# Tiles of x for layer 1 kept beside the projection's tiles and asked for earlier

## The chip, the cores and the metric

The kernel runs on one core of a Trainium2 chip. The metric is the time of one execution on the device in microseconds; the median of five executions is given, and one more was profiled. The core has five engines with queues of their own: PE (TensorE, matmuls, with PEld for its weight loads), DVE (VectorE), ACT (ScalarE), POOL (GpSimd) and SP (SyncE, here only a queue from which transfers are issued). Transfers are also issued from ACT and POOL; all of them share 16 DMA engines.

## The reference

The input x is one image of 48 channels by 256 x 256. Two layers, each adding to x what it computes from a group-normalised x (`_gn`: 16 groups of 3 channels, mean and variance over the whole image).

```
# layer 0
qkv = dwconv3x3(einsum('bchw,oc->bohw', _gn(x), w_qkv))     # 144 channels
q, k, v = heads(split(qkv))        # 4x4 patches: 8 heads, 96 values per patch
attn = softmax(l2norm(q)^T l2norm(k) * temperature)         # 4356 x 4356 per head, padding's border included
x = x + einsum(fold(v attn^T), w_proj)                      # the projection
# layer 1
xb = _gn(x) cut into windows of 64 x 64
x = x + einsum('bcphqw,twW,thH,tcC->bCpHqW', xb, Ws, Hs, Cs)   # t = 0, 1, 2
```

## The kernel before

All data are float32. Layer 0 goes through statistics of x, the pointwise and depthwise convolutions and the attention of eight heads; that takes the first 3227 of 3705 us. Attention's matmuls lie in a hand-ordered loop. At its end the sums of the last head are transposed and stored to DRAM in the tensor `os_` (`store`, L609 to L619, from POOL), which has 16 parts; each covers 256 patches.

**The projection** (L726 to L762) goes over 8 tiles t. One tile takes 16 rows of the upper half of the image and 16 rows of the lower half, on 96 partitions. For each tile SP loads `pot` (`os_`, parts t and 8 + t, L740) and `pxt` (x itself, L741), two loads each, 768 KB apiece. PE multiplies `pot` with the projection weights (L746), DVE adds the result onto `pxt` (L753) and takes statistics of it (L757), and POOL stores the rows to `x1s` in DRAM (L762, two stores). `pot` and `pxt` have three buffers each, in the pool `pj`. Behind the loop come the group statistics for layer 1, then its channel weights `csn` scaled by them (L782) and a bias `cbias` (L788).

**Layer 1** goes over 8 units: a unit is one row of windows (64 image rows) by one half of the image's width (128 columns). For each unit `load_x` loads `lxq` (two loads of 768 KB from `x1s`, 32 rows each on 48 partitions, L815) and `load_rows` loads the same data once more in another layout for the residual (`lrt`, L824). `over_c` (L828) contracts the channels on PE (L841); DVE subtracts `cbias` and writes the tile `lzt` (L848). `over_w` contracts the width with `wsb` (L863), `over_h` the height with `hsb` (L880), `residual` adds (L892) and stores to the output (L895). The units are worked on in a hand-ordered block: `load_x` for units 0 and 1 and `over_c(0)` first, then each unit with `load_x` of the unit after next and `over_c` of the next one woven into it.

**Order.** Instructions outside the hand-ordered blocks are put into an order on each engine's queue by a planner: one that is ready goes, and among several ready ones the one written earlier. On its queue each instruction then waits for the semaphores that it needs.

**Places in SBUF.** Pools are stacked in the order in which they are opened; a pool that has been closed leaves its place to later ones, and a first tile there waits for those who used it. Per partition: attention had `cv` (52 KB), `ahead` with the key, query and value tiles (80 KB), then the pool of the `e` tiles (48 KB), then small ones. In their place the projection opens `l1c` (1 KB), `pj` (`pot` 48 KB, then `pxt` 48 KB) and `pjs` (3 KB). When these two are closed, layer 1 opens `lx` (48 KB, three `lxq`), `lz` (`wsb`, `hsb`, two `lzt`; 74 KB), `lr` (24 KB) and `ly` (24 KB) from the same address on as `pj`: `lxq` lies on `pot`, `wsb` and the first `lzt` on `pxt`.

Of the kernel before, what the change touches and what calls it, by code (L numbers as in the profile page):

```python
# [8 lines left out]
F32 = mybir.dt.float32  # L9
# [4 lines left out]
PSUM = bass.MemoryType.PSUM  # L14
DRAM = bass.MemoryType.DRAM

C = 48
H = W = 256
# [23 lines left out]
WS = 64  # L42
# [3 lines left out]
def conv_preact_kernel(  # L46
# [15 lines left out]
    nc = tc.nc  # L62
# [16 lines left out]
    x1s = dram.tile([C, H, W], F32, name="x1s")  # L79
# [18 lines left out]
    for s in range(2):  # L98
        r = slice(s * C, (s + 1) * C)
        for h in range(NH if s == 0 else H0):  # L100
            o = s * M0 + h * HC if h < H0 else (h - H0) * HC
            nc.gpsimd.dma_start(
                out=(wq[r] if h < H0 else wr[0:C])[:, o : o + HC].rearrange("c (z e) -> c z e", z=3),
                in_=w_qkvT.rearrange("c (z h e) -> h c z e", z=3, h=NH)[h],
# [22 lines left out]
    def group_stats(st, mean, rstd, pool, pspool):  # L127

        mv = pool.tile([P2, 2], F32, name="mv")
        nc.vector.bn_aggr(mv, st.rearrange("p n s -> p (n s)"))  # L130
        pm = pspool.tile([P2, 1], F32, name="pm", tag="pstat")
        nc.tensor.matmul(pm, lhsT=gm, rhs=mv[:, 0:1], start=True, stop=True)
        nc.vector.tensor_copy(mean, pm)
        d = pool.tile([P2, 1], F32, name="gsd")
        nc.vector.tensor_sub(d, mv[:, 0:1], mean)
        e = pool.tile([P2, 1], F32, name="gse")
        nc.vector.scalar_tensor_tensor(e, d, d, mv[:, 1:2], ALU.mult, ALU.add)
        pv = pspool.tile([P2, 1], F32, name="pv", tag="pstat")
        nc.tensor.matmul(pv, lhsT=gm, rhs=e, start=True, stop=True)
        f = pool.tile([P2, 1], F32, name="gsf")  # L140
        nc.vector.tensor_scalar_add(f, pv, EPS)
        g = pool.tile([P2, 1], F32, name="gsg")
        nc.scalar.activation(g, f, AF.Sqrt)
        nc.vector.reciprocal(rstd, g)
        return mv, e
# [257 lines left out]
    with tc.tile_pool(name="xn", bufs=1) as xnp, tc.tile_pool(name="cst", bufs=1) as cst, tc.tile_pool(  # L403
        name="nps", bufs=2, space=PSUM
# [7 lines left out]
        parts = [16] * 7 + [8, 4, 4]  # L412
        st0 = cst.tile([P2, HALF * W // 512, 6], F32, name="st0")
        for i, LR in enumerate(parts):
            j = sum(parts[:i])
            for s in range(2):
                eng = nc.sync if s == 0 else nc.scalar
                eng.dma_start(
                    out=xr[s * C : (s + 1) * C, j : j + LR, :], in_=xc[:, s * HALF + j : s * HALF + j + LR, :]
# [70 lines left out]
    with tc.If(nc.values_load(large) > 0):  # L490
# [8 lines left out]
        with tc.tile_pool(name="mk", bufs=NM) as mk, tc.tile_pool(name="mq", bufs=2) as mq, tc.tile_pool(  # L499
            name="mps", bufs=2, space=PSUM  # L500
# [23 lines left out]
    with tc.tile_pool(name="ahead", bufs=2) as ah, tc.tile_pool(name="ae", bufs=3) as ae, tc.tile_pool(  # L524
        name="asm", bufs=6
# [109 lines left out]
        with tc.manual_schedule():  # L635
            load_query(0, 1)
            block = scores(0, 0)
            for h in range(NH):
                more = h + 1 < NH
                rows = {r: Depthwise(h + 1, r) for r in range(CR + 1)} if more else {}  # L640
                for g in range(NG):
# [57 lines left out]
                    for k in range(NK):  # L699
                        s = (h * NG + g) * NK + k  # L700
# [25 lines left out]
    l1c = ctx.enter_context(tc.tile_pool(name="l1c", bufs=1))  # L726
    RP = TP // PX * KS
    NP = TP
    with tc.tile_pool(name="pj", bufs=3) as pj, tc.tile_pool(name="pjs", bufs=1) as pjs, tc.tile_pool(
        name="pps", bufs=3, space=PSUM  # L730
    ) as pps, tc.tile_pool(name="pp1", bufs=1, space=PSUM) as pp1:
        st1 = pjs.tile([P2, HALF * W // 512, 6], F32, name="st1")
        ov = os_.rearrange("t (c k) n -> t c k n", k=KK)
        for t in range(HALF // RP):
            ot = pj.tile([P2, KK, NP], F32, name="pot")
            xt = pj.tile([P2, RP, W], F32, name="pxt")
            for s in range(2):
                r = slice(s * C, (s + 1) * C)
                y0 = s * HALF + t * RP
                nc.sync.dma_start(out=ot[r], in_=ov[s * (NT // 2 // TP) + t])  # L740
                nc.sync.dma_start(out=xt[r], in_=xc[:, y0 : y0 + RP, :])  # L741
            xv = xt.rearrange("p (py ki) (px kj) -> p ki kj py px", ki=KS, kj=KS)
            for ki in range(KS):
                ps = pps.tile([P2, KS, NP], F32, name="pps")
                for i in range(0, KS, 2):
                    nc.tensor.matmul(  # L746
                        ps[:, i : i + 2, :],
                        lhsT=wp,
                        rhs=ot[:, ki * KS + i : ki * KS + i + 2, :],
                        start=True,  # L750
                        stop=True,
                    )
                nc.vector.tensor_add(  # L753
                    xv[:, ki], ps.rearrange("p k (py px) -> p k py px", py=RP // KS), xv[:, ki]
                )
            for i in range(0, RP, 2):
                nc.vector.bn_stats(  # L757
                    st1[:, (t * RP + i) // 2, :], xt[:, i : i + 2, :].rearrange("p a b -> p (a b)")
                )
            for s in range(2):  # L760
                y0 = s * HALF + t * RP
                nc.gpsimd.dma_start(out=x1s[:, y0 : y0 + RP, :], in_=xt[s * C : (s + 1) * C])  # L762

        gm2 = pjs.tile([P2, 64 + C], F32, name="gm2")
        nc.vector.memset(gm2, 0.0)
        for o in (0, 64):
            nc.vector.tensor_copy(gm2[:, o : o + C], gm[:, 0:C])
        mv1, e1 = group_stats(st1, mean1, rstd1, pjs, pp1)
        pc1 = pp1.tile([64 + C, 1], F32, name="pc1", tag="pstat")
        nc.tensor.matmul(pc1, lhsT=gm2, rhs=e1, start=True, stop=True)  # L770
        rstd2 = l1c.tile([64 + C, 1], F32, name="rstd2")
        nc.vector.tensor_scalar_add(rstd2, pc1, EPS)
        nc.scalar.activation(rstd2, rstd2, AF.Sqrt)
        nc.vector.reciprocal(rstd2, rstd2)

        csn = l1c.tile([64 + C, T3 * C], F32, name="csn")
        for s in range(2):
            nc.scalar.dma_start(
                out=csn[s * 64 : s * 64 + C].rearrange("c (t d) -> c t d", t=T3), in_=Cs.rearrange("t c d -> c t d")
            )  # L780
            r = slice(s * 64, s * 64 + C)
            nc.vector.tensor_scalar_mul(csn[r], csn[r], rstd2[r])  # L782
        mrow = pjs.tile([C, 128], F32, name="mrow")
        nc.vector.tensor_scalar_mul(mrow, ones, mean1[0:C])
        pb1 = pp1.tile([128, T3 * C], F32, name="pb1")
        nc.tensor.matmul(pb1, lhsT=mrow, rhs=csn[0:C], start=True, stop=True)
        cbias = l1c.tile([128, T3 * C], F32, name="cbias")
        nc.vector.tensor_copy(cbias, pb1)  # L788


    with tc.tile_pool(name="lx", bufs=3) as lx, tc.tile_pool(name="lz", bufs=2) as lz, tc.tile_pool(
        name="lr", bufs=2
    ) as lr, tc.tile_pool(name="ly", bufs=4) as ly, tc.tile_pool(name="ps1", bufs=2, space=PSUM) as ps1, tc.tile_pool(
        name="ps2", bufs=2, space=PSUM
    ) as ps2, tc.tile_pool(name="ps3", bufs=1, space=PSUM) as ps3:
        wsb = lz.tile([128, T3, 128], F32, name="wsb", bufs=1)
# [2 lines left out]
        for s in range(2):  # L799
            r = slice(s * WS, (s + 1) * WS)  # L800
            nc.scalar.dma_start(out=wsb[r, :, r], in_=Ws.rearrange("t w v -> w t v"))
            nc.scalar.dma_start(out=hsb[r], in_=Hs.rearrange("t h g -> h t g"))
        HW = WS // 2
        units = [(yw, xh) for yw in range(H // WS) for xh in range(2)]
        NQ = 3
        xqs, rts, zts, blks, parts = {}, {}, {}, {}, {}

        def load_x(u):

            yw, xh = units[u]  # L810
            xcol = slice(xh * 128, (xh + 1) * 128)
            xq = lx.tile([64 + C, HW, 128], F32, name="lxq")
            for s in range(2):
                y0 = yw * WS + s * HW
                nc.sync.dma_start(out=xq[s * 64 : s * 64 + C], in_=x1s[:, y0 : y0 + HW, xcol])  # L815
            xqs[u] = xq

        def load_rows(u):

            yw, xh = units[u]  # L820
            xcol = slice(xh * 128, (xh + 1) * 128)
            rt = lr.tile([128, NQ * 8, 128], F32, name="lrt")
            for s in range(2):
                nc.sync.dma_start(  # L824
                    out=rt[s * WS : (s + 1) * WS],
                    in_=x1s[s * 24 : (s + 1) * 24, yw * WS : (yw + 1) * WS, xcol].rearrange("c y x -> y c x"),
                )
            rts[u] = rt  # L828

        def over_c(u):  # L830
# [3 lines left out]
            zv = zt.rearrange("p k (s y) -> p s y k", s=2)  # L834
            for y0 in range(0, HW, 3):
                n = min(3, HW - y0)
                pa = ps1.tile([128, 2, 512], F32, name="pa")
# [62 lines left out]


        with tc.manual_schedule():
            for u in range(2):
                load_x(u)
            for _ in over_c(0):
                pass
            late = None
            for u in range(len(units)):
                load_rows(u)
                if u + 2 < len(units):  # L910
                    load_x(u + 2)
                ahead = over_c(u + 1) if u + 1 < len(units) else iter(())
                for q in range(NQ):
                    parts[u, q] = []
                    for b in range(2):
                        c0 = b * 24 + q * 8
                        parts[u, q].append(over_w(u, c0, c0 + 4))
                        for _ in range(2):
                            next(ahead, None)
                    if late:  # L920
                        over_h(*late)
                    late = u, q
            over_h(*late)
# [41 lines left out]
```

## Time and profile before

| | us |
|---|---|
| median of 5 executions | 3707.51 (3693.68 to 3708.61) |
| the profiled execution, its own time | 3707.05 |
| its span, first to last instruction | 3705.1 |
| PE busy | 3466.3 (94%) |
| PEld / DVE / ACT / POOL busy | 2906.9 / 2140.5 / 1874.2 / 542.8 |
| statistics to attention | 0 to 3227 |
| projection | 3227 to 3392 |
| layer 1 up to its first matmul over the width | 3392 to 3427 |
| rest of layer 1 | 3427 to 3705 |

Times inside the execution are microseconds from the span's start. A row of the timeline gives start, length, engine, line, operation, written tile <- read tiles, count, and in brackets how long the engine was idle before and who ended that. "SPq" is the issuing of a transfer on SP: the data land later. The chain that ended last is followed back from the last instruction, at each step to what released it. A DMA share of 1.00 means that all 16 DMA engines are busy on average; it can read somewhat above 1.

### The profile page before, as it was taken

The page shows a single profiled execution, that of the slowest core. Times are in us where ns is not written, and L with a number is a line of the kernel's source. Part 1 is how long each engine was busy: PE and PEld are TensorE (multiplying, and loading weights), DVE is VectorE, ACT ScalarE, POOL GpSimd, SP SyncE. Part 2 cuts the span into 40 slices and gives each one's busy share as a digit, 9 for nine tenths or more (in the row PEclk, how much of TensorE's full clock was granted, in tenths as well). Part 3 has the DMA queues.
Part 4 walks back from the last instruction along what each step waited for, and adds up shares of the span by engine and source line. Part 5 has one row for each costly group of instructions (what it writes and reads, how often), then busy time and mean ns, then how long its engine had stood idle before and what let it go on. Part 6 is the DMA issues. An engine that isn't in the chain of part 4 may idle for free.

```text
span 3705.1 us, 100318 instructions
## 1 busy us (share of the span) xinstructions
PE 3466.3 (94%) x44252; PEld 2906.9 (78%) x44252; DVE 2140.5 (58%) x3514; ACT 1874.2 (51%) x2747; POOL 542.8 (15%) x628
## 2 busy tenths in 40 slices
PE   2878999999999999999999999999999999855998
PEld 1337787889988888998888989888888888712776
DVE  5464774179628953894399349925982222266564
ACT  0245675666546664665566556655664444300332
POOL 2030111012211211121122112201220000000011
PEclk9989999999999999999999999999999999966999
DMA  7455665533323332333233323332333100299774
GB/s 155 157 128 152 178 177 160 153 95 92 96 77 84 93 85 79 82 90 96 72 91 87 86 73 93 86 88 83 94 81 84 36 19 19 56 247 191 126 139 92
DMA packets 274146, 386.48 MB, mean 104 GB/s; under 512 B 77010, under 2 KB 211522, under 8 KB 269480
## 3 DMA queue, kind: packets, MB, share of 16 engines
q1 hardware_dynamic: 234790, 264.95, 27.4%
q0 software_dynamic: 35424, 106.40, 12.3%
q10 hardware_dynamic: 3490, 8.64, 1.2%
q8 instruction: 350, 5.73, 0.6%
q14 instruction: 92, 0.75, 0.1%
HBM read 234.76 MB, written 144.90 MB: 102 GB/s over the span
## 4 chain that ended last, share of the span: by engine, by line
PE 82%; DMA 5%; issue 2%; DVE 2%; ACT 1%; SPq 0%; POOL 0%; ACTq 0%; POOLq 0%; DVEq 0%
PE big L337 36%; PE big L595 35%; PE pb L863 4%; PE pa L841 2%; PE pc L880 2%; DMA x1s<-pxt 1%; DVE acc L228 1%; PE big L177 1%; DMA pxt<-in_x_dram 1%; PE pt L612 1%; PE pn L247 1%; DMA t<-ot 1%; PE pst L549 1%; DMA kt<-qkv 1%; DMA pad<-t 0%
## 5 line engine op out<-in xcount | busy, mean ns | idle before, releaser
L566 ACT ACTIVATE e<-big,nmx 128x1024 f32<-128x1024 f32 x1024 | 1144.0, 1118 | 877.0 <-PE big L337 612.8
L337 PE MATMUL big<-kt,qt 128*128 128x512 f32 x6144 | 1437.9, 393 | 34.2 <-DMA kt<-qkv 29.9
L595 PEld LDWEIGHTS big<-vn,e 128*64 128x64 f32 x32768 | 1357.0, 137 | 57.6 <-ACT e L566 30.6
L595 PE MATMUL big<-vn,e 128*64 128x96 f32 x32768 | 1387.3, 247 | 6.4 <-DVE oacc L606 2.8
L337 PEld LDWEIGHTS big<-kt,qt 128*128 128x128 f32 x6144 | 1145.8, 188 | 282.6 <-issue 32.8
L606 DVE TENSOR_TENSOR oacc<-big,oacc 128x768 f32<-128x768 f32 x480 | 453.6, 954 | 711.1 <-PE big L595 711.1
L228 DVE SCALAR_TENSOR_TENSOR acc<-pad,dwt,acc 126x1024 f32<-126x1024 f32 x592 | 765.6, 1293 | 39.1 <-DMA pad<-t 18.8
L579 DVE TENSOR_REDUCE zt<-zs 128x1 f32<-128x4 f32 x256 | 38.5, 150 | 339.5 <-ACT e L566 339.5
L295 POOL DMA_DIRECT2D qkv<-o x72 | 52.8, 734 | 1238.6 <-ACT o L279 1238.6
L289 POOL TENSOR_TENSOR ol<-o,oh 126x1024 fp32r<-126x1024 f32 x78 | 184.9, 2371 | 311.9 <-DVE ss L243 238.9
L566 ACT ACTIVATION_READ_ACCUMULATOR e<-big,nmx 128x1 f32 x1024 | 195.6, 191 | 0.0
L848 DVE TENSOR_TENSOR lzt<-pa,cbias 128x864 f32<-128x864 f32 (+1 forms) x88 | 136.9, 1628 | 98.1 <-PE pa L841 98.1
L870 ACT COPY lyt<-pb 128x512 f32<-128x512 f32 x144 | 84.5, 587 | 214.0 <-PE pb L863 214.0
L279 ACT COPY o<-acc 126x1024 f32<-126x1024 f32 x74 | 159.2, 2152 | 0.0
L863 PEld LDWEIGHTS pb<-wsb,lzt 128*64 128x64 f32 x2304 | 126.2, 138 | 27.6 <-issue 19.5
L616 POOL DMA_DIRECT2D os__70<-oo x128 | 65.2, 515 | 541.7 <-ACT oo L614 541.5
L863 PE MATMUL pb<-wsb,lzt 128*64 128x128 f32 x2304 | 142.2, 280 | 1.3 <-issue 1.3
L746 PE MATMUL pps<-pot,wp 96*96 96x512 f32 x128 | 76.8, 768 | 65.5 <-DMA pot<-os__70 65.5
L239 ACT ACTIVATE sq<-acc 126x1024 f32<-126x1024 f32 x74 | 78.3, 1059 | 101.5 <-DVE acc L228 101.5
L180 ACT ACTIVATE ot<-big,bias 108x1024 f32<-108x1024 f32 x64 | 68.1, 1111 | 113.3 <-PE big L177 60.9
L209 ACT ACTIVATE acc<-pad,dwt 126x1024 f32<-126x1024 f32 x74 | 84.2, 1138 | 81.2 <-DMA pad<-t 81.2
L746 PEld LDWEIGHTS pps<-pot,wp 96*96 96x96 f32 x128 | 26.5, 215 | 115.3 <-issue 104.3
(124 smaller groups left out, 1979.4 us busy)
## 6 DMA issues: line engine op xcount, KB each, us to landing
pad<-t SPq DMA_DIRECT2D x238, 254.0 KB
t<-ot SPq DMA_DIRECT2D x128, 217.7 KB
qkv<-ol POOLq DMA_DIRECT2D x78, 336.0 KB, 6.2
qkv<-oh POOLq DMA_DIRECT2D x70, 336.0 KB, 5.5
qt<-qkv SPq DMA_DIRECT2D x176, 96.0 KB
xs<-in_x_dram SPq DMA_DIRECT2D x128, 96.0 KB
os__70<-oo POOLq DMA_DIRECT2D x128, 96.0 KB, 2.1
pxt<-in_x_dram SPq DMA_DIRECT2D x16, 768.0 KB
```

Of the source, the lines that this page charges most:

```text
L209: nc.scalar.mul(self.acc, self.pad[:, 0:KS, 0:W], dwt[:, self.h, 0:1])
L228: nc.vector.scalar_tensor_tensor(self.acc, self.pad[:, dy : dy + KS, dx : dx + W], dwt[:, self.h, tap : tap + 1], self.acc, ALU.mult, ALU.add,
L279: nc.scalar.copy(self.o.rearrange("p (a b) x -> p a b x", a=KS), self.acc.rearrange("p a (x b) -> p a b x", b=KS))
L289: eng.tensor_sub(self.ol, self.o, self.oh.bitcast(F32))
L337: nc.tensor.matmul(ps[:, i, :], lhsT=qt[:, r, q0 : q0 + 128], rhs=kts[2 * j + i][:, r // 2, :], start=(r == 0), stop=(r == 2),)
L566: nc.scalar.activation(e[:, j * 1024 : (j + 1) * 1024], ps.rearrange("p a b -> p (a b)"), AF.Exp, bias=nmx[:, b : b + 1], accum_out=zs[:, ...
L595: nc.tensor.matmul(ps[p : p + 64, j // 4, j % 4 * HD : (j % 4 + 1) * HD], lhsT=e[:, mb * 128 + p : mb * 128 + p + 64], rhs=vn, start=(i == 0),
L606: nc.vector.tensor_add(oaccs[h, k], ps[:, :, : 4 * HD], oaccs[h, k])
L746: nc.tensor.matmul(ps[:, i : i + 2, :], lhsT=wp, rhs=ot[:, ki * KS + i : ki * KS + i + 2, :], start=True, stop=True,)
L848: nc.vector.tensor_tensor(zv[:, :, y0 : y0 + n, :], pa[:, :, : n * T3 * C].rearrange("p s (y k) -> p s y k", y=n), cbias.rearrange("p (u v ...
L863: nc.tensor.matmul(pb[s * WS : (s + 1) * WS, i, :], lhsT=zts[u][:, t * C + c + i, :], rhs=wsb[:, t, :], start=True, stop=True,)
L870: nc.scalar.copy(yt[:, t, :], pb.rearrange("p i x -> p (i x)"))
```

## The change

The pool `lx` and `load_x` move up, ahead of `pj`, and `lx` stays open to the end of the kernel. So `lxq` gets a place of its own (where `pot` was), `pj` and `pjs` lie 48 KB higher while they are open, and `lz`, `lr` and `ly` keep their addresses. The calls `load_x(0)` and `load_x(1)` move from the head of layer 1's hand-ordered block to the end of the projection's loop, ahead of the group statistics, so the planner places them.

```diff
@@ -726,6 +726,22 @@
     l1c = ctx.enter_context(tc.tile_pool(name="l1c", bufs=1))
     RP = TP // PX * KS
     NP = TP
+
+    lx = ctx.enter_context(tc.tile_pool(name="lx", bufs=3))
+    HW = WS // 2
+    units = [(yw, xh) for yw in range(H // WS) for xh in range(2)]
+    xqs = {}
+
+    def load_x(u):
+
+        yw, xh = units[u]
+        xcol = slice(xh * 128, (xh + 1) * 128)
+        xq = lx.tile([64 + C, HW, 128], F32, name="lxq")
+        for s in range(2):
+            y0 = yw * WS + s * HW
+            nc.sync.dma_start(out=xq[s * 64 : s * 64 + C], in_=x1s[:, y0 : y0 + HW, xcol])
+        xqs[u] = xq
+
     with tc.tile_pool(name="pj", bufs=3) as pj, tc.tile_pool(name="pjs", bufs=1) as pjs, tc.tile_pool(
...
@@ -760,6 +776,8 @@
             for s in range(2):
                 y0 = s * HALF + t * RP
                 nc.gpsimd.dma_start(out=x1s[:, y0 : y0 + RP, :], in_=xt[s * C : (s + 1) * C])
+        for u in range(2):
+            load_x(u)
 
         gm2 = pjs.tile([P2, 64 + C], F32, name="gm2")
...
@@ -788,9 +806,7 @@
-    with tc.tile_pool(name="lx", bufs=3) as lx, tc.tile_pool(name="lz", bufs=2) as lz, tc.tile_pool(
-        name="lr", bufs=2
-    ) as lr, tc.tile_pool(name="ly", bufs=4) as ly, tc.tile_pool(name="ps1", bufs=2, space=PSUM) as ps1, tc.tile_pool(
+    with tc.tile_pool(name="lz", bufs=2) as lz, tc.tile_pool(name="lr", bufs=2) as lr, tc.tile_pool(name="ly", bufs=4) as ly, tc.tile_pool(name="ps1", bufs=2, space=PSUM) as ps1, tc.tile_pool(
...
@@ -800,20 +816,8 @@
-        HW = WS // 2
-        units = [(yw, xh) for yw in range(H // WS) for xh in range(2)]
         NQ = 3
-        xqs, rts, zts, blks, parts = {}, {}, {}, {}, {}
-
-        def load_x(u):
...
-            xqs[u] = xq
+        rts, zts, parts = {}, {}, {}
...
@@ -900,8 +904,6 @@
         with tc.manual_schedule():
-            for u in range(2):
-                load_x(u)
             for _ in over_c(0):
                 pass
```

More of the change, by code (lines that the diff above doesn't have):

```diff
@@ L802, in conv_preact_kernel @@
             nc.scalar.dma_start(out=hsb[r], in_=Hs.rearrange("t h g -> h t g"))
-        HW = WS // 2
-        units = [(yw, xh) for yw in range(H // WS) for xh in range(2)]
         NQ = 3
-        xqs, rts, zts, blks, parts = {}, {}, {}, {}, {}
-        def load_x(u):
[L810 to L815, printed above, removed]
-            xqs[u] = xq
+        rts, zts, parts = {}, {}, {}
         def load_rows(u):
```

## The prediction

> **What bounds the kernel now.** I read the page first: the tensor engine is busy 94% of the span, so nearly every stage is a matmul stage and a change to loads can only matter where that engine waits. The row of 40 slices shows one such place, slices 36 and 37, between attention and layer 1. The chain that ended last, for that stretch, says what it waits for (start us, length us, what):
>
> ```profile
> 3328.26 20.55 DMA pxt<-in_x_dram
> 3348.88 18.17 issue
> 3367.07 0.69 POOL x1s L762 x2
> 3367.76 15.05 issue
> 3383.32 8.77 DMA x1s<-pxt
> 3392.64 14.26 DMA lxq<-x1s
> 3407.04 1.79 PE pa L841 x11
> 3408.85 1.63 DVE lzt L848
> ```
>
> The reader is to see the handover: the projection's last store of x1s lands at 3383.32 + 8.77 = 3392.1, only then is layer 1's first tile of x asked for, it takes 14.26 us, and the first matmuls of layer 1 follow. These 14.26 us are the only thing that the change can win.
>
> Next, what SP's queue waited for (total us, times, longest), from 3205 to 3420:
>
> ```profile
> SPq L741 <- DMA x1s<-pxt: 84.7, 5, 22.6
> SPq L815 <- DMA x1s<-pxt: 43.6, 2, 28.5
> SPq L741 <- DVE vn L585: 42.3, 1, 42.3
> ```
>
> Unit 0 reads rows 0 to 63 of x1s, which the projection's tiles 0 to 3 wrote; tile 3's store was issued at 3310.0. Yet its load (L815) sits until the store of tile 7 has landed. It waits for a place in SBUF: lxq lies where pot lay, and a pool's first tile waits until all of the closed pool under it is done with. The third row shows the same rule at the other end: the projection's first load (L741, an input, no data to wait for) waited for vn, the last instruction to read vT, a tile of attention's pool "ahead" that lies 20 KB above anything pxt covers.
>
> Third, how full the DMA engines are (stretch, length, PE, PEld, DVE, ACT, POOL busy, TensorE clock, DMA share, GB/s):
>
> ```profile
> 3216.00:3228.00 12.00, 12.00 (x254) 11.40 (x254) 3.30 (x6) 1.66 (x4) 2.03 (x4) 1.00 0.77 167
> 3228.00:3240.00 12.00, 3.73 (x36) 2.87 (x32) 0.96 (x1) 2.12 (x4) 4.39 (x9) 0.79 0.69 149
> 3240.00:3368.00 128.00, 67.86 (x112) 23.35 (x112) 84.64 (x81) 1.86 (x2) 8.71 (x18) 0.69 1.01 250
> 3368.00:3376.00 8.00, 4.86 (x7) 1.85 (x8) 3.38 (x5) 0.00 (x0) 0.08 (x1) 0.57 0.79 258
> 3376.00:3383.00 7.00, 4.08 (x10) 1.30 (x8) 7.00 (x5) 0.00 (x0) 0.18 (x1) 0.91 0.00 1
> 3383.00:3392.00 9.00, 1.49 (x6) 1.24 (x6) 7.16 (x16) 0.23 (x2) 0.83 (x2) 0.50 0.68 175
> 3392.00:3407.00 15.00, 1.66 (x4) 1.00 (x4) 1.44 (x6) 0.18 (x1) 0.00 (x0) 0.50 1.10 135
> ```
>
> From 3240 to 3368 the DMA engines are full (1.01): the projection is bound by its transfers. They are idle only from 3376 to 3383, and partly beside the last two stores. Last, the timeline where attention ends:
>
> ```profile
> 3215.99 0.79 SPq L741 DMA_DIRECT2D pxt<-in_x_dram  x2
> 3227.09 11.79 SPq L740 DMA_DIRECT2D pot<-os__70  x3
> 3228.71 0.83 PEld L612 LDWEIGHTS pt<-ident,oacc 128*96 128x96 f32 x8
> 3235.25 1.07 ACT L614 COPY oo<-pt 96x512 f32<-96x512 f32 x2 [6.78 <-DMA os__70<-oo]
> 3244.86 8.94 PE L746 MATMUL pps<-pot,wp 96*96 96x512 f32 x16 [7.03 <-DMA pot<-os__70]
> ```
>
> **The change, part by part.** No instruction is added or taken away: the four loads of units 0 and 1 (768 KB each) are issued earlier, and pools move. Each effect is costed apart.
>
> *Units 0 and 1 are asked for earlier (gain).* They have no SBUF wait left, and their data are there: SP issues its last projection load at 3347.8, and tile 3's store, issued at 3310.0, landed before SP went on at 3328.3. They are written behind the projection's loads, and from tile 3 on the timeline has those on SP in their written order (pot, pxt, pot, pxt), so I put them behind. They enter the same queue after tile 7's loads, which are in by 3371.1 (first matmul of tile 7). What can it win at most? csn is ready at 3393.0, PE is free of the bias matmul at 3393.6, one group of matmuls takes 1.79 us: DVE could start at 3395.4 instead of 3408.85, 13.4 us. Do the tiles arrive by then? In the stretch after 3392, 135 GB/s move 1.57 MB for unit 0 and 0.2 MB for wsb and hsb in 13.1 us: 5.8 us for one load, 11.6 for unit 0. Free DMA time from 3371.1 to 3393.6 is 1.5 (of 3371 to 3376) + 7.0 + 9 x 0.32 = 2.9, in all 11.4: just enough if the stores lose nothing. But lz, with wsb and the tile lzt that DVE writes, lies on pj still, so DVE's memset of wsb and then L848 wait for the last store. If store and loads share evenly, its 8.8 us become about 13, it lands at 3396.5 and DVE starts at 3397.2: 11.6 us won. If the store takes twice its time (17.6, landing 3400.9) it is 7.2. If the loads get nothing beside it, unit 0 lands near 3395.2 and DVE starts at 3397: 11.8. I take 11, near the two middle readings; the ends are 7 and 13.4.
>
> The row for this sharing: beside the stores from 3370 to 3393 their queue moved 245 packets with 2.97 MB, 12 KB each, while x's loads after 3393 run at 7440 packets for 3.78 MB, 0.5 KB each. The Trainium skill, DMA: Bandwidth & Descriptors, section Queues, rings and completion order, says that each engine takes turns between the queues, a whole packet at a time. By that the store with its large packets would hardly slow (landing near 3392.5), and the sum below would be some 2 us better, 3697.5; no run here has shown the two together.
>
> *The other loads of the handover.* wsb and hsb (ACT's queue) are issued after the memset. hsb's first load was issued at 3393.6, and SP's wait for it ended at 3406.6: 13 us. From a memset at 3397 wsb lands near 3411; the first matmul on it comes 18.4 us (3427.3 - 3408.85) after DVE's first, at 3415.5: covered by 4 us; without that cover the gain falls by what is missing. lrt for unit 0 is behind unit 1 on SP, and on the store; it is read at 3450.7 before, at 3440 after, and its 11.6 us end by 3420. Unit 2's load and what follows move with the stage. Nothing is costed.
>
> *The projection's tiles lie 48 KB higher (loss).* From the pools' sizes: cv takes 52 KB, ahead 80, the e tiles 48. pj (96 KB) covered cv and part of ahead; with lx under it, it reaches 14 KB into the e tiles' pool. Those are free when the last weighted sum has been taken, which the transposes at 3228.71 follow; so the first load of pj can go at 3228.7, not at 3215.99. Only its rule (a whole pool) is needed, not which tile lies on what. Its own delay, 12.7 us, isn't the price: DVE reads pxt at 3248.75. The first projection matmul waits for pot's second half, and this for attention's third group of os stores. Two loads (1.57 MB, 6.3 us at 250 GB/s) leave an open stretch for one with 0.31 x 12 = 3.7 us free, so at least 2.6 us are pushed on into the full stage. And the os stores now run beside three loads instead of one: the second group took 6.37 us beside one load against 4.14 for the first; if it waits until the loads are through, at about 3228.7 + 3 x 3.15 = 3238.2 against 3235.2, the third group, the second half of pot and the first matmul are 3 to 3.5 us late. I take 3.5. The ends: 0 (if only the tile that lies on e waits, pxt's third, wanted after 3241 anyway) and 6.3 (all of it added).
>
> *gm2, mrow and the small tiles* move into e's region with pj; they are read at 3391 and later. Nothing. Their memset on DVE comes after the last sums instead of before: 0.4 us where DVE has 3 us of work in 12.
>
> **Sum.** The profiled execution took 3707.05 us (span 3705.1 and 1.95 around it), 0.5 below the median 3707.51 of the five. 3707.05 - 11 + 3.5 = 3699.5, 0.2% below. From no change a measurement here can tell about 0.3%, 11 us: five runs lie between 3693.68 and 3708.61.
>
> **Rivals.**
> *Start unharmed.* Only the waiting tile is late, and the full 13 are won: 3694. For it: pxt's 24 us of slack to 3248.75. Against: the wait for vn shows whole pools.
> *Nothing won.* x's loads still wait for the last store, because x1s is held as one tensor. Then 3.5 is lost: 3710.5. Against: pot's first load at 3227.09 went while most of os was not stored yet, so parts are told apart.
> *Slower: x before the tiles.* Nothing but readiness orders SP's queue outside the hand-ordered loops; rows 0 to 31 are ready after tile 1's store. If the four loads go out ahead of tile 7's (or earlier ones), 4 x 5.8 = 23.2 us stand in a stretch with share 1.01, and the ring of three pxt buffers passes them on; 13.4 are won at the end, 3.5 lost at the start: +13.3, 3720.4. It decides where the first of them stands before the last load of pxt. For it: pxt's first two went ahead of pot's, against the written order. Against: there pot's data were late; later, tile by tile, pot and pxt alternate as written.
>
> **How the numbers follow.** Forecast 0.52 (its own range 3695 to 3704), start unharmed 0.20, nothing won 0.11, x before the tiles 0.12, other 0.05. 3692 to 3714 leaves out the slower rival and the tails, 0.18. Faster by over 0.3% means below 3696: most of the second case and a sixth of the first, 0.26. Slower, above 3718.5: most of the third rival, and what I can't name, 0.16. Else 0.58.
>
> **What would show it.** Right: x's loads on SP directly behind the last of pxt (near 3350); the wait for lxq gone or under 3 us; the first L848 some 1.5 to 5 us behind the last store's landing; that store taking 9 to 13 us; the first pxt issued near 3229, waiting for PE or os; the first pps matmul 2 to 4 us later than 3244.86. Wrong: x's loads among the tiles'; a new wait for wsb at the first L863; the store at 17 us or more.

## The result, and the profile after

The changed kernel takes 3695.6 us in the median of 48 runs (3681.59 to 3712.23), the kernel before 3700.1 us in 88 (3689.3 to 3710.4). The ratio is 0.9987, with a 95% interval of 0.9981 to 0.9992: 4.8 us faster (3.0 to 7.0), within the 0.3% that the forecast calls no change. The profiled execution took 3703.55 us (span 3701.7). The wider set puts the kernel before 7 us under the five runs that the forecast started from, so its 3699.5 is to be read as the difference of its sum: -7.5 us, against -4.8 here.

The line numbers move: in the changed kernel pot is loaded at L756, pxt at L757, lxq at L742; the projection's matmul is L762, its store L778, csn L800, the memset of wsb L813, lrt L828, pa L845, lzt L852, pb L867. First the chain that ended last, after, at the handover (start us, length us, what):

```profile
3358.46 23.84 DMA pot<-os__70
3382.43 5.97 PE pps L762 x8
3388.42 5.78 DVE pxt L769 x3
3394.20 4.76 DVE st L773 x8
...
3404.08 0.30 DVE csn L800
3404.42 0.61 PE pb L804
3405.03 1.71 PE pa L845 x11
3406.76 1.65 DVE lzt L852
```

The store and the 14.26 us wait for lxq are gone from it. The chain now comes through the last tile's load, its matmuls, the statistics and csn; PE's first matmul of layer 1 follows straight away. From csn's first multiplication (3404.08) to DVE's first subtraction (3406.76) it is 2.68 us; before it was 3408.85 - 3392.41 = 16.44 (the row of csn before is shown below). What ends last here is no longer a transfer of x but the statistics.

The timeline, after, around the last load of the projection and the last store (columns as before):

```profile
3358.91 0.42 SPq L757 DMA_DIRECT2D pxt<-in_x_dram  x1
3359.38 37.34 SPq L742 DMA_DIRECT2D lxq<-x1s  x4
3394.49 1.00 POOL L778 DMA_DIRECT2D x1s<-pxt  x2 [15.16 <-DVE pxt L769]
3405.91 3.01 SPq L828 DMA_DIRECT2D lrt<-x1s  x2
3405.98 0.38 DVE L813 MEMSET wsb<- 128x384 f32 x1 [0.37 <-DMA x1s<-pxt]
```

The four loads of x stand directly behind the last pxt, as forecast. SP was busy with issuing them for 37.34 us: unit 0's second load occupied it from 3359.96 to 3386.47, so unit 1's were issued at 3386.51 and 3392.28, and the last of them still runs beside the store. lrt on SP and the memset on DVE both wait for the last store: its second part, issued at 3394.99, landed at 3405.79, 10.8 us (8.77 before). DVE waited 0.37 us for it.

The stretches, after (columns as before):

```profile
3222.00:3234.00 12.00, 12.00 (x240) 11.40 (x238) 2.87 (x3) 2.23 (x4) 3.69 (x8) 0.95 0.15 43
3234.00:3246.00 12.00, 2.72 (x28) 1.84 (x22) 1.35 (x4) 1.16 (x2) 2.38 (x5) 0.76 0.97 161
3250.00:3380.00 130.00, 69.42 (x112) 23.71 (x112) 85.63 (x82) 0.75 (x1) 8.33 (x17) 0.68 1.01 255
3384.00:3394.50 10.50, 7.81 (x15) 2.60 (x13) 8.09 (x5) 0.00 (x0) 0.01 (x1) 0.83 1.00 257
3394.50:3406.00 11.50, 3.07 (x17) 2.82 (x19) 8.41 (x21) 0.41 (x2) 0.99 (x2) 0.50 1.04 245
```

Two things are to be seen in the DMA share (last but one). The idle 7 us behind tile 7 are filled (1.00). And the 12 us before the last weighted sums end carry 0.15 where they carried 0.77: that capacity is lost, and the DMA engines then start the full stretch with more to do. That loss is in the timeline where attention ends:

```profile
3234.35 1.08 PE L612 MATMUL pt<-ident,oacc 128*96 128x128 f32 x8
3234.57 0.30 SPq L756 DMA_DIRECT2D pot<-os__70  x1
3234.92 0.42 SPq L757 DMA_DIRECT2D pxt<-in_x_dram  x1
3248.13 0.30 SPq L756 DMA_DIRECT2D pot<-os__70  x1
3248.39 1.07 ACT L614 COPY oo<-pt 96x512 f32<-96x512 f32 x2 [11.62 <-DMA os__70<-oo]
3254.05 6.26 PE L762 MATMUL pps<-pot,wp 96*96 96x512 f32 x7 [16.59 <-DMA pot<-os__70]
```

No load of the projection goes before the last weighted sum. ACT waits 11.62 us for the os stores that run beside these loads (6.78 before), and pot's second half and the first matmul wait for those.

**How the profiles are compared.** This profile's attention ends 5.6 us later than that of before (third transposes 3234.35 against 3228.71). That is chance: in three profiles of one and the same program (below) the last weighing starts at 3231.56, 3224.96 and 3215.68, and nothing in front of it differs. So from here on every time is counted from the start of the last weighing, the last 64 matmuls of attention's weighted sums (L595, 3225.92 before and 3231.56 after). "Early" is the number of pxt's 768 KB loads that SP issued ahead of it; "second tile" is the first projection matmul of tile 1. From the timelines, first before, then after:

```profile
3225.92 2.86 PE L595 MATMUL big<-vn,e 128*64 128x96 f32 x64
3258.91 10.44 PE L746 MATMUL pps<-pot,wp 96*96 96x512 f32 x16 [5.11 <-DMA pot<-os__70]
3382.82 1.01 POOL L762 DMA_DIRECT2D x1s<-pxt  x2 [14.75 <-DVE pxt L753]
3392.41 0.62 DVE L782 TENSOR_SCALAR csn<-csn,rstd 48x144 f32<-48x144 f32 x2
```

```profile
3231.56 2.86 PE L595 MATMUL big<-vn,e 128*64 128x96 f32 x64
3271.95 10.01 PE L762 MATMUL pps<-pot,wp 96*96 96x512 f32 x16 [7.48 <-DMA pot<-os__70]
```

| kernel | early | first projection matmul | second tile | last store | csn | DVE's first lzt | from first pb to the end |
|---|---|---|---|---|---|---|---|
| before | 2 | 18.9 | 33.0 | 156.9 | 166.5 | 182.9 | 277.8 |
| before, again | 2 | 18.9 | 33.7 | 156.5 | 166.1 | 183.0 | 277.6 |
| changed | 0 | 22.5 | 40.4 | 162.9 | 172.5 | 175.2 | 276.5 |
| changed, again | 0 | 22.4 | 40.3 | 159.2 | 168.8 | 171.5 | 278.6 |
| call back (same program) | 0 | 22.9 | 40.7 | 164.3 | 173.9 | 176.5 | 278.2 |
| place alone | 0 | 22.4 | 39.6 | 156.9 | 166.5 | 182.2 | 277.1 |
| two buffers | 2 | 19.3 | 33.3 | 158.0 | 167.6 | 171.4 | 281.1 |
| unit 0 alone | 2 | 17.1 | 31.3 | 154.7 | 164.3 | 167.0 | 281.0 |
| pxt below | 3 | 22.0 | 30.9 | 152.3 | 161.9 | 166.7 | 277.5 |
| x before tile 7 | 0 | 23.1 | 40.9 | 184.2 | 193.8 | 196.5 | 278.3 |
| pxt at the bottom | 6 | 22.4 | 32.7 | 146.4 | 156.0 | 171.7 | 276.7 |
| shared ring | 6 | 22.5 | 31.7 | 143.0 | 152.6 | 155.3 | 277.9 |

The changed program's three rows give the balance: the last store 162.1 in the mean against 156.7, a loss of 5.4 us; from csn to DVE 2.7 instead of 16.4 us (16.8 in the second profile of before), a gain of 13.7; the rest of layer 1 equal (277.8 against 277.7). Together -8.3 us. The three sets of times of that same program say -4.8 (-7.0 to -3.0), -9.6 (-13.7 to -5.6) and -10.0 us (-14.1 to -5.6); weighted by their intervals that is -6.4. They scatter more than their intervals allow, and no run here says why; the interval of the first, from 48 runs, does not reach the -7.5 of the forecast's sum, the other two hold it.

### The profile page after: what moved, and what is told of

It is laid out like the page before. It is cut to its first block, busy times and chain, and to the rows that moved or that the text cites. A ratio compares the mean times of both kernels' runs of the same rounds, so it can differ in the third digit from the quotient of the medians.

```text
span 3701.7 us, 100308 instructions
## 1 busy us (share of the span) xinstructions
PE 3468.0 (94%) x44252; PEld 2908.2 (79%) x44252; DVE 2140.1 (58%) x3514; ACT 1872.8 (51%) x2747; POOL 541.7 (15%) x628
## 3 DMA queue, kind: packets, MB, share of 16 engines
q0 software_dynamic: 35424, 106.40, 12.3%
## 4 chain that ended last, share of the span: by engine, by line
PE 83%; DMA 5%; DVE 2%; issue 1%; ACT 1%; SPq 1%; ACTq 0%; POOL 0%; POOLq 0%; DVEq 0%
PE big L337 37%; PE big L595 35%; PE pb L867 4%; PE pa L845 2%; PE pc L884 2%; DMA pot<-os__70 1%; PE big L177 1%; DMA x1s<-pxt 1%; DMA t<-ot 1%; PE pt L612 1%; PE pn L247 1%; DVE acc L228 1%; PE pst L549 1%; DMA pxt<-in_x_dram 1%; DMA kt<-qkv 0%
## 5 line engine op out<-in xcount | busy, mean ns | idle before, releaser
L595 PEld LDWEIGHTS big<-vn,e 128*64 128x64 f32 x32768 | 1358.6, 137 | 57.6 <-ACT e L566 30.6
L595 PE MATMUL big<-vn,e 128*64 128x96 f32 x32768 | 1388.9, 247 | 6.4 <-DVE oacc L606 2.5
L852 DVE TENSOR_TENSOR lzt<-pa,cbias 128x864 f32<-128x864 f32 (+1 forms) x88 | 137.0, 1629 | 82.8 <-PE pa L845 82.8
L279 ACT COPY o<-acc 126x1024 f32<-126x1024 f32 x74 | 159.2, 2151 | 0.0
L762 PE MATMUL pps<-pot,wp 96*96 96x512 f32 x128 | 78.8, 785 | 75.5 <-DMA pot<-os__70 75.5
L867 PEld LDWEIGHTS pb<-wsb,lzt 128*64 128x64 f32 x2304 | 125.2, 138 | 27.6 <-issue 17.9
L867 PE MATMUL pb<-wsb,lzt 128*64 128x128 f32 x2304 | 141.1, 278 | 1.2 <-DVE lzt L852 1.2
L762 PEld LDWEIGHTS pps<-pot,wp 96*96 96x96 f32 x128 | 27.0, 218 | 126.8 <-issue 92.0
```

What stands on the lines that cost most here:

```text
L279: nc.scalar.copy(self.o.rearrange("p (a b) x -> p a b x", a=KS), self.acc.rearrange("p a (x b) -> p a b x", b=KS))
L595: nc.tensor.matmul(ps[p : p + 64, j // 4, j % 4 * HD : (j % 4 + 1) * HD], lhsT=e[:, mb * 128 + p : mb * 128 + p + 64], rhs=vn, start=(i == 0),
L762: nc.tensor.matmul(ps[:, i : i + 2, :], lhsT=wp, rhs=ot[:, ki * KS + i : ki * KS + i + 2, :], start=True, stop=True,)
L852: nc.vector.tensor_tensor(zv[:, :, y0 : y0 + n, :], pa[:, :, : n * T3 * C].rearrange("p s (y k) -> p s y k", y=n), cbias.rearrange("p (u v ...
L867: nc.tensor.matmul(pb[s * WS : (s + 1) * WS, i, :], lhsT=zts[u][:, t * C + c + i, :], rhs=wsb[:, t, :], start=True, stop=True,)
```

## The experiments

Differences in us are the ratio's distance from 1, times the kernel before on the same chip (3700.91, 3701.67 and 3703.53 us in the three groups of runs). The place alone and pxt at the bottom are edits of the kernel before, the others of the changed kernel.

**The place alone.** An empty 48 KB pool under `pj`, in the kernel before; `lx` is opened behind `lz`, so that it still lies on `pj`.

```diff
-    with tc.tile_pool(name="pj", bufs=3) as pj, tc.tile_pool(name="pjs", bufs=1) as pjs, tc.tile_pool(
+    with tc.tile_pool(name="gap", bufs=1) as gap, tc.tile_pool(name="pj", bufs=3) as pj, tc.tile_pool(name="pjs", bufs=1) as pjs, tc.tile_pool(
...
+        gap.tile([128, 3 * 32 * 128], F32, name="gap")
...
-    with tc.tile_pool(name="lx", bufs=3) as lx, tc.tile_pool(name="lz", bufs=2) as lz, tc.tile_pool(
+    with tc.tile_pool(name="lz", bufs=2) as lz, tc.tile_pool(name="lx", bufs=3) as lx, tc.tile_pool(
```

> The start alone: the kernel before, with an empty 48 KB place under pj, so that the projection's tiles lie where the change puts them; lxq still lies on pj and is asked for after the last store, as before. Theory (pj's pool now reaches into the e tiles' pool, the first loads go only when the last weighted sum is taken): first pxt issued at the end of the last weighing instead of some 13 us ahead of it, first projection matmul 19 to 20 us behind the last weighing instead of 16.15, another 2 to 3 us in the first tiles, so +6 us against before in all (+0.16%). Rival 'start unharmed' (the later start in the changed kernel's profile is chance): 0. Rival 'attention's end suffers too' (all of the 11.3 us by which tile 7 is later in the profile belongs to the place): +9 to +11 us, the last weighing itself later against the stages before it. Handover (wait for lxq, 14 us) as before in all three.

Ratio 1.0011 (1.0002 to 1.0019): 4.1 us slower (0.7 to 7.0). "Start unharmed" falls, and so does "attention's end suffers too". In the timeline of this kernel (lines one higher than before):

```profile
3218.34 2.86 PE L595 MATMUL big<-vn,e 128*64 128x96 f32 x64
3221.35 0.30 SPq L741 DMA_DIRECT2D pot<-os__70  x1
3221.70 0.42 SPq L742 DMA_DIRECT2D pxt<-in_x_dram  x1
3234.95 0.30 SPq L741 DMA_DIRECT2D pot<-os__70  x1
3240.78 9.52 PE L747 MATMUL pps<-pot,wp 96*96 96x512 f32 x16 [12.45 <-DMA pot<-os__70]
```

the first loads go at the end of the last weighing and pot's second half 13.6 us behind, as in the changed kernel; the first matmul is 22.4 us behind the last weighing's start, 3.5 later than before. The second tile starts 39.6 us behind the mark, as late as in the changed program (40.3 to 40.7), where the four profiles with two early loads have 31.3 to 33.7. Then, in this one execution, the tiles caught up (last store 156.9). The four profiles without an early load and without x among the tiles have their last store between 156.9 and 164.3: from the second tile to the last one's first matmul they take 104.5 to 111.8 us, those with two early loads 111.1 to 112.5. So the later tiles take back between nothing and 8 us, and no run here says why; one profile decides the loss at the last store no better than to 4 us.

**Two buffers for lxq.** Then `pj` ends below the pool of the e tiles.

```diff
-    lx = ctx.enter_context(tc.tile_pool(name="lx", bufs=3))
+    lx = ctx.enter_context(tc.tile_pool(name="lx", bufs=2))
```

> The changed kernel with two buffers for lxq instead of three (32 KB): pj then ends below the e tiles' pool, and units 0 and 1 are still asked for behind the projection's loads. Theory: the start is as before (pxt's first two loads ahead of the last weighing, first projection matmul 16 us behind it), the handover as in the changed kernel (first pa right behind csn, 13.8 us won): 13 us faster than before (-0.35%), 8 us faster than the changed kernel. Rival 'start unharmed': like the changed kernel, -5 us. Rival 'a third buffer is needed in layer 1' (unit 2's load now waits until over_c of unit 0 is done): the rest of layer 1 longer than 276 to 278 us, the gain smaller by that much.

Ratio 0.9971 (0.9963 to 0.9980): -10.7 us. The timeline at the start of this kernel

```profile
3218.95 0.79 SPq L757 DMA_DIRECT2D pxt<-in_x_dram  x2
3248.18 9.37 PE L762 MATMUL pps<-pot,wp 96*96 96x512 f32 x16 [6.91 <-DMA pot<-os__70]
```

is that of before again (19.3 us to the first matmul, 33.3 to the second tile), so the late start comes from the pool's reach into the e tiles. The handover stays won (3.8 us from csn to DVE; the last store takes 12.3 us here, and DVE waits 1.85 for it). The third expectation came true as well: 281.1 us behind the first pb against 276.5 to 278.6 in all kernels with three buffers. SP waited 47.3 us for over_c there (4.6 in the second profile of the changed kernel). How that turns into 3 us on PE was not followed.

**The call put back.** `load_x` for units 0 and 1 is called at the head of the hand-ordered block again; the place stays.

```diff
-        for u in range(2):
-            load_x(u)
...
         with tc.manual_schedule():
+            for u in range(2):
+                load_x(u)
```

> The changed kernel with the calls of load_x for units 0 and 1 back at the head of the hand-ordered block; only lxq's place is changed against before. Theory (what held the loads was the place alone, SP has nothing else between): SP issues them behind the last pxt all the same, time and profile like the changed kernel, -3 to -7 us against before. Rival (where the call is written matters, the loads go behind csn's and the weights' or wait for the block): handover wait of several us comes back, 0 to +9 us against before, since the start's loss stays.

The profiles of the two kernels hold the same instructions on every engine, waits included, and on SP's queue in the same order: they are one program. Moving the call from the end of the loop to the head of the block does nothing; only the place does. Ratio 0.9973 (0.9962 to 0.9985): a second set of times of the changed program.

**pxt below, pot on top.** Pools of their own, so that only pot's reaches into the e tiles.

```diff
-    with tc.tile_pool(name="pj", bufs=3) as pj, tc.tile_pool(name="pjs", bufs=1) as pjs, tc.tile_pool(
+    with tc.tile_pool(name="pj", bufs=3) as pj, tc.tile_pool(name="po", bufs=3) as po, tc.tile_pool(name="pjs", bufs=1) as pjs, tc.tile_pool(
...
-            ot = pj.tile([P2, KK, NP], F32, name="pot")
+            ot = po.tile([P2, KK, NP], F32, name="pot")
```

> The changed kernel with pxt and pot in pools of their own, pxt's 48 KB below, pot's on top, so that only pot's pool reaches into the e tiles' pool. Theory (a pool's first tile waits for whoever used any closed pool under it; pxt going late beside os's stores is the loss): pxt's first loads go ahead of the last weighing again, pot's first half when the last weighing is done (1.5 us later than before); start loss 0 to 2 us, handover as in the changed kernel: -11 to -13 us against before. Rival (the loss comes from something else than pxt's first loads): like the changed kernel, -3 to -7 us.

Ratio 0.9966 (0.9953 to 0.9979): -12.6 us. The time came out as the theory had it, but not by its steps. From the timeline of this kernel:

```profile
3210.73 2.55 SPq L757 DMA_DIRECT2D pxt<-in_x_dram  x3
3226.89 1.07 ACT L614 COPY oo<-pt 96x512 f32<-96x512 f32 x2 [7.63 <-DMA os__70<-oo]
3227.53 1.65 PE L612 MATMUL pt<-ident,oacc 128*96 128x128 f32 x8 [2.34 <-ACT oo L614]
3244.32 14.39 PE L762 MATMUL pps<-pot,wp 96*96 96x512 f32 x28 [7.05 <-DMA pot<-os__70]
```

Three loads of pxt go early, the os stores are slow beside them, even PE's transposes wait, and the first matmul is as late as in the changed kernel (22.0). Yet the last store comes at 152.3, 4.4 us sooner than before. So the first matmul's delay alone is not the loss. The last store follows how many loads were done ahead of the stretch whose DMA engines are full: none early gives 156.9 to 164.3 (mean 160.8), two 154.7 to 158.0 (156.5), three 152.3. The first two ranges touch, and three stands on one profile; the second tile parts them better (39.6 to 40.9, 31.3 to 33.7, 30.9). The store takes 13.3 us here, DVE waits 2.83 for it, and of the handover's gain 2.1 are lost (4.8 us from csn to DVE).

**The changed kernel again, and the kernel before again.**

> The changed kernel once more, beside the runs below on one chip. Theory (a loss of 3.5 us at the start and 2.5 in the first tiles, 13.8 won at the handover): 6 to 8 us faster than before; the part of the profile ahead of the last weighing is chance and will differ by several us again, while the distances behind the last weighing's start stand within 2 us: first projection matmul 22.5 (18.9 before), last store 163 to 164 (156.9), DVE's first subtraction 175 to 177 (182.9). Rival (the 5.6 us by which attention ends later in the first profile belong to the change): attention's end later again than in the profile of before by 4 to 6 us.

> The kernel before once more, for a second profile of it. Theory: time as before within the interval; distances behind the start of the last weighing as in the first profile within 3 us: first projection matmul 18.9, last store 156.9, first subtraction 182.9. Rival (the 156.9 is one lucky execution, the changed kernel's tiles lose nothing): last store 160 to 163.

0.9974 (0.9963 to 0.9985) and 1.0003 (0.9991 to 1.0016). The distances of before repeat within 0.7 us (156.9 and 156.5 to the last store), those of the changed program only within 5, where 2 were expected; attention's end in the second profile of the changed kernel is earlier, not later. Two profiles of before are few to say that its tiles scatter less.

**Unit 0 alone early.** One buffer for unit 0 under `pj`, two for the others on top of where `pj` was.

```diff
-    lx = ctx.enter_context(tc.tile_pool(name="lx", bufs=3))
+    lx = ctx.enter_context(tc.tile_pool(name="lx", bufs=1))
...
-        xq = lx.tile([64 + C, HW, 128], F32, name="lxq")
+        xq = (lx if u == 0 else lx1).tile([64 + C, HW, 128], F32, name="lxq")
...
-        for u in range(2):
-            load_x(u)
+        load_x(0)
...
-    with tc.tile_pool(name="lz", bufs=2) as lz, tc.tile_pool(name="lr", bufs=2) as lr, tc.tile_pool(name="ly", bufs=4) as ly, tc.tile_pool(name="ps1", bufs=2, space=PSUM) as ps1, tc.tile_pool(
+    with tc.tile_pool(name="lx1", bufs=2) as lx1, tc.tile_pool(name="lz", bufs=2) as lz, tc.tile_pool(name="lr", bufs=2) as lr, tc.tile_pool(name="ly", bufs=4) as ly, tc.tile_pool(name="ps1", bufs=2, space=PSUM) as ps1, tc.tile_pool(
...
         with tc.manual_schedule():
+            load_x(1)
```

> Only unit 0 is asked for early: a place of one buffer (16 KB) for unit 0 under pj, the tiles of the other units in two buffers that lie on pj, so that unit 1's loads wait for the last store as before. pj ends below the e tiles' pool, so the start is as before. Theory (beside the stores, each load of x stretches them; with two loads gone by then instead of four the last store has the DMA engines nearly to itself): last store lands 8.8 to 9.5 us after its issue instead of 11, first pa right behind csn; the handover gains 13 to 14 us, -13 us against before in all. Rival (the landing is set by the store's own size): landing 11 us as in the changed kernel, same time as with two buffers early, -10 us. Rival (unit 1 is late for its over_c): a wait of several us for lxq later in layer 1, rest of layer 1 over 280 us.

Ratio 0.9979 (0.9965 to 0.9994): -7.8 us (-13.0 to -2.2). The store's landing is seen from unit 1's loads, which wait for it (timeline):

```profile
3373.15 1.00 POOL L778 DMA_DIRECT2D x1s<-pxt  x2 [16.19 <-DVE pxt L769]
3382.58 1.09 SPq L742 DMA_DIRECT2D lxq<-x1s  x2
```

The second part, issued at 3373.65, landed 8.7 us later, as without any load beside it (8.77, 8.63 and 8.65 in before, before again and the place alone); unit 0's loads were all but through, SP's queue moved 0.09 MB of them beside the store's 1.57. With four loads asked for it took 10.8, 10.5 and 11.2 us in the changed program (1.24 MB beside the store in the first), 12.3 with two buffers and 13.3 with pxt below. So the first theory holds: loads of x stretch the store. The gain fell short of -13; this version has two buffers for the other units and loses the same 3 us in layer 1 (281.0), and the interval is too wide to say whether that is all.

**x ahead of tile 7.** The slower rival as a kernel of its own.

```diff
             xt = pj.tile([P2, RP, W], F32, name="pxt")
+            if t == 7:
+                for u in range(2):
+                    load_x(u)
...
-        for u in range(2):
-            load_x(u)
```

> The changed kernel with the loads of units 0 and 1 written ahead of tile 7's loads, so that SP issues them there. Prices the slower rival. As the prediction has it (23.2 us of x loads in a stretch where the DMA engines are full push tile 7's loads back by as much): first matmul of tile 7 some 20 us later than in the changed kernel against tile 6's, +13 us against before. Other reading (the DMA engines' work is the same and only changes places; the idle 7 us and the half-empty stretch behind tile 7 are lost): tile 7 later by 12 to 16 us, handover as in the changed kernel, +2 to +8 us against before. If the loads go out long before tile 7 is wanted: as the changed kernel.

Ratio 1.0033 (1.0016 to 1.0049): 12.2 us slower (5.9 to 18.1). The timeline of the matmuls of tiles 6 and 7, and the stretch between:

```profile
3357.91 10.45 PE L765 MATMUL pps<-pot,wp 96*96 96x512 f32 x16 [9.21 <-DMA pot<-os__70]
3397.36 9.50 PE L765 MATMUL pps<-pot,wp 96*96 96x512 f32 x16 [29.00 <-DMA pot<-os__70]
```

```profile
3358.00:3397.00 39.00, 10.36 (x16) 3.39 (x16) 12.47 (x12) 0.00 (x0) 1.00 (x2) 0.59 1.01 227
```

Tile 7 starts 39.45 us behind tile 6; in the changed kernel it was 3382.43 - 3364.58 = 17.85. That is 21.6 us for four loads of x, 5.4 each, at a share of 1.01.

**pxt at the bottom, loads early, handover as before.** cv, the pool under it, is done with long before attention ends.

```diff
-    with tc.tile_pool(name="pj", bufs=3) as pj, tc.tile_pool(name="pjs", bufs=1) as pjs, tc.tile_pool(
+    with tc.tile_pool(name="px", bufs=3) as px, tc.tile_pool(name="pj", bufs=3) as pj, tc.tile_pool(name="pjs", bufs=1) as pjs, tc.tile_pool(
...
-            xt = pj.tile([P2, RP, W], F32, name="pxt")
+            xt = px.tile([P2, RP, W], F32, name="pxt")
```

> The kernel before with pxt alone at the bottom, on attention's first pool, and pot above it; layer 1 as before, its lxq on both, asked for after the last store. It prices the loads ahead of the last weighing alone. Theory (each load of pxt that goes out before the last weighing takes its 3.1 us out of the full stretch; six go early instead of two): last store 144 to 145 behind the last weighing's start instead of 156.9, handover as before (DVE 16.4 us behind csn), -12 us against before, so that the run with the shared ring is this and the handover's 13 us together. Rival (the gains do not add, part of the ring's 24 us comes from the two together): -6 to -9 us or -15 to -18 us.

Ratio 0.9958 (0.9945 to 0.9972): -15.6 us (-20.4 to -10.4), without any change at the handover (15.8 us from csn to DVE). The last store comes at 146.4, and the profile's parts make -12.2: the last store 10.3 sooner, 0.9 at the handover, 1.0 in the rest. The times do not decide between the theory (-12) and the rival in which the gains do not simply add (-15 to -18): the interval holds both.

**A shared ring.** pxt at the bottom, and lxq in its three buffers: unit 0 follows the store of tile 5, unit 1 that of tile 6, unit 2 that of tile 7.

```diff
-    lx = ctx.enter_context(tc.tile_pool(name="lx", bufs=3))
+    px = ctx.enter_context(tc.tile_pool(name="px", bufs=3))
...
-        xq = lx.tile([64 + C, HW, 128], F32, name="lxq")
+        xq = px.tile([64 + C, HW, 128], F32, name="lxq", tag="px")
...
-            xt = pj.tile([P2, RP, W], F32, name="pxt")
+            xt = px.tile([64 + C, RP, W], F32, name="pxt", tag="px")[0:P2]
```

> pxt lies alone at the bottom (where only attention's first pool, cv, was), pot above it, and lxq takes its turn in the same three buffers as pxt (both take 16 KB), so units 0, 1 and 2 follow the stores of tiles 5, 6 and 7; lz, lr and ly lie above, as before. All six first loads of pxt can go while attention still runs, when the DMA engines are a tenth busy. Theory (the projection's end is set by the transfers that lie between the last weighing and tile 7; four loads of 3.1 us fewer): last store 12 us earlier behind the last weighing's start than before (145 against 156.9); handover as in the changed kernel (first pa within 1 us behind csn, DVE 3 to 4 us behind csn), so -24 to -26 us against before. Rival (the os stores and pot's way set the pace, not the loads): first projection matmul and tiles as before, -12 to -14 us. Rival (unit 0 waits for tile 5's store and comes late): a wait of up to 5 us for lxq, -20 us.

Ratio 0.9935 (0.9920 to 0.9950): 24.1 us faster than before (18.5 to 29.6), 3679.37 us in the median, the best version here. Where pxt's early loads went, and the handover (the tile's operations, then the timeline):

```profile
L757 SPq DMA_DIRECT2D pxt<-in_x_dram x6: 328/502/582, 2781.9 to 2832.5; - x6
```

```profile
3359.80 1.00 POOL L778 DMA_DIRECT2D x1s<-pxt  x2 [16.20 <-DVE pxt L769]
3369.39 0.61 DVE L800 TENSOR_SCALAR csn<-csn,rstd 48x144 f32<-48x144 f32 x2
3370.95 0.38 DVE L813 MEMSET wsb<- 128x384 f32 x1
3372.07 3.10 DVE L852 TENSOR_TENSOR lzt<-pa,cbias 128x864 f32<-128x864 f32 x2 [0.74 <-PE pa L845]
```

All six loads went between 2781.9 and 2832.5, in a stretch in which PE stayed busy for 60.00 of 60 us (2780 to 2840, DMA share 0.70; 0.36 in the same stretch of before). DVE follows csn by 2.68 us, and the memset no longer waits for a store, since wsb lies on pot and not on pxt. Against the run without the handover's part this is 8.5 us less by the times and 16.4 by the profiles (155.3 against 171.7 to DVE's first lzt); the handover's own 13.7 lies between, so whether the two gains simply add stays open.

## Why the prediction was right or wrong

**The sum.** -7.5 us in its terms, -8.3 in the profiles of the changed program and -6.4 in its times. The direction is right, and the time stays within 0.3%. Both terms were too small; that the two errors nearly cancel in the sum is luck.

**The gain, 11 us.** 13.7, above its upper end of 13.4, because PE puts layer 1's first matmul between the two of the bias and DVE starts 2.7 us behind csn instead of 3.0. The step that was mis-sized is the store beside the loads: the forecast took a landing near 3396.5, 13 us (even sharing), and let DVE wait for it. It took 10.5 to 11.2, and as csn comes 9.6 us behind the store's issue (166.5 - 156.9), and PE and DVE need 2.7 more, hardly any of it shows: DVE's first subtraction is 1.0 us behind the landing, where the forecast's sign was 1.5 to 5. The mechanism is there, though: in the two versions whose store took 12.3 and 13.3 us, DVE did wait for it. The Trainium skill, DMA: Bandwidth & Descriptors, section Queues, rings and completion order, has each engine take turns between queues, a whole packet at a time. The forecast's reading of it, a landing near 3392.5, would be 9.2 us; the changed program lies between that and the 13 us of even sharing, and the store took 8.6 to 8.8 us with no load beside it or one unit's nearly through, 10.5 to 13.3 with two units' asked for.

**The start, 3.5 us.** The first matmul is 3.5 us late in every profile of the changed program (3.5 to 3.9) and in the place alone (3.5), by the mechanism named: the whole pool waits, the os stores run beside the loads. But the price is the wrong quantity. The second tile is 7.4 us late in the mean of the four profiles without an early load (40.3 against 32.8 with two, and the two groups do not overlap), more than the upper end of 6.3 that the forecast worked out as "all of it added": two loads of 3.15 us. The later tiles take part of that back, by amounts that differ between executions of one program (105.9 to 111.8 us from the second tile to the last one's first matmul), and the last store is 5.4 us late in the mean of the changed program (2.5 to 7.6). pxt below points the same way, with a first matmul just as late and tiles that end sooner than before. The forecast had the sentence that mattered (two loads leave an open stretch for a full one) and then priced the first matmul instead. The place alone costs 4.1 us in its times (0.7 to 7.0), which bears out a loss but not its size, and its own profile has none left at the last store.

**What costs nothing.** The first pb comes 18.4 us behind DVE's first subtraction in both kernels (3425.19 - 3406.76 after), so wsb's loads are covered. The memset of gm2 did move behind the last sums on DVE, and is on no chain.

**The rivals.** "Start unharmed" is refuted by the place alone. "Nothing won" is refuted by the chain. "x before the tiles" was rightly priced: +13.3 forecast, +12.2 measured, 21.6 us in the tiles for the 23.2 expected. It did not come about, because the loads stand behind the last pxt.

## What to carry to other kernels

In a stretch whose DMA engines are full, don't price the first late instruction: count the transfers that are moved out of the stretch or into it. From none to six early loads the last store moves from 160.8 to 144.7 us in the means of four and of two profiles, 2.7 us a load, where 768 KB at 250 GB/s are 3.15; the same count comes near the loss here and led to the version that wins 24 us. And before a tile is moved to be asked for earlier, look at which closed pool lies under it and when that one is done with: choosing the neighbour that ends first (cv alone, where before pj lay on cv and ahead and the change put it up to the e tiles) was worth more than the change itself, 15.6 us against 6.4.

## What the runs showed that was not expected

- A pool's place alone decided when the loads go; moving the call from the loop's end to the head of layer 1's block decided nothing (two sources, one program). Ahead of tile 7's loads, the call's place does decide: that kernel is 12.2 us slower than before.
- Loads of x cost 5.4 us apiece in the full stretch, loads of pxt 2.7 to 3.15, for the same 768 KB. In the stretch with x SP's queue moved 5486 packets for 5.78 MB (1.1 KB each, x's and the others' together), with pot and pxt alone 1655 for 20.33 MB (12 KB each, before, 3250 to 3368), at the same share of 1.01. No run here changes the packets alone, so that they are the cause is not shown.
- Attention's end lies between 3215.7 and 3231.6 us in three executions of one program: 16 us, more than anything the change does. Without a common mark in the trace the two first profiles would have shown a loss at the start twice as large as it is.
